# Attention sums made in a row, and softmax reciprocals spread by TensorE instead of GpSimd

## The chip, the cores and the metric

One core of one Trainium2 chip runs the whole program. The metric is the time of one execution on the device in microseconds (us), as the median of several runs. Engines are named as in the profile: PE is TensorE's matrix product, PEld its weight load, DVE is VectorE, ACT is ScalarE, POOL is GpSimd, SP is SyncE, whose queue issues transfers.

## The reference, cut to what matters

The input x has shape (4, 1024, 256). Four blocks are added to it one after the other, each on a layer norm of x: a linear recurrent unit, a sparse feed-forward block (the same weights are used twice), an attention block, and the feed-forward block again. The change lies in the attention:

```
q = (x @ Wq.T).reshape(b, t, 8, 64)
kv_latent = x @ Wkv_down.T
k = (kv_latent @ Wk_up.T).reshape(b, t, 8, 64)
v = (kv_latent @ Wv_up.T).reshape(b, t, 8, 64)
scores = einsum('bqhd,bkhd->bhqk', q, k) * 64 ** -0.5
attn = softmax(scores, axis=-1)
out = einsum('bhqk,bkhd->bqhd', attn, v)
return out.reshape(b, t, 512) @ Wo.T
```

Everything is float32. The output is x after all four blocks.

## The kernel before, in words

x stays in SBUF as 32 tiles of 128 tokens by 256. The program has three stages. Up to about 390 us it runs the recurrent unit, prepares the attention's weights and starts the first feed-forward block; from 392 to 1310 us it runs the attention, with the rest of the first feed-forward block (L589) and the preparation of later queries, keys and outputs woven in; then the second feed-forward block ends the program.

**Units of the attention.** `heads` (L857) goes over one batch in 32 units: two halves of the tokens (`nb`), four pairs of heads (`g`), four query tiles (`q`). With four batches that is 128 units. A unit has two steps, one for each head of the pair (`j`). A step makes scores of 128 queries by 1024 keys on TensorE (L887, four records), copies them with the sign turned into SBUF on VectorE while it takes the row minimum (L893, tile `pr`, four buffers; `nm` is the bias), and takes exponentials with their row sums on ScalarE (L896, row sums to `ssum`). The probabilities must then be transposed, so that keys lie on partitions.

**Two ways to transpose.** A DMA unit (`q` even) splits the probabilities into two float16 parts, by a cast on ScalarE (L899) and a difference on POOL (L900), in tile `pd` (two buffers), and SP issues a transposing transfer to `d0` or `d1` (L901, two buffers each). A TensorE unit (`q` odd) transposes float32 blocks on TensorE (L907) and copies them from PSUM to `p0` or `p1` (L912, mostly ScalarE, one buffer each).

**The sum of a unit.** `values_sum` (L922) is called later for a unit that is done. It takes reciprocals of the two row sums (L926, VectorE), spreads them over 2 x 64 columns on POOL (L928, `rows`), multiplies the transposed probabilities with the values on TensorE (L932: 48 records with float16 `lb` for a DMA unit, 32 records with float32 `la` for a TensorE unit), transposes `rows` (L940) into the second half of the same PSUM tile `pmo`, copies that half to `rb` (L942, ScalarE, one buffer) and multiplies both halves into `on` (L943, VectorE). `pmo` shares the two PSUM buffers of tag "s" with all products that are woven in. `rs`, `rows` and most small tiles come from a pool with two buffers.

**What sets the order.** `heads` keeps finished units in two lists. A TensorE unit is summed in step j == 0 of the unit after it, a DMA unit in step j == 1 of the next DMA unit. After each step `merge` (L965) lets woven-in work run by due times written by hand (L1189 to L1216). Tile's planner then orders the instructions of each engine by a simulated timeline; buffers and data become waits on semaphores. So each engine has one fixed order of instructions, which is known from the built program, and a waiting instruction holds up those behind it on its engine.

The functions that the change touches, with what calls them:

Of the kernel before, what the change touches and what calls it, by code (L numbers as in the profile page):

```python
# [10 lines left out]
F32 = mybir.dt.float32  # L11
# [10 lines left out]
P = 128  # L22
B = 4
# [7 lines left out]
HD = 64  # L31
PAIRS = HEADS // 2
# [741 lines left out]
class Attention:  # L774
# [82 lines left out]
    def heads(self, b, psum):  # L857

        nc, sp, wp = self.nc, self.sp, self.hp
        kh, kl, la, lb = self.k[b]
        late, pending = [], []
        for nb, g, q in (
            (nb, g, q)
            for nb in range(2)
            for g in range(PAIRS)
            for q in ((0, 2, 1, 3) if b == B - 1 and nb and g == PAIRS - 1 else range(4))
        ):
            by_dma = q % 2 == 0  # L870
            if g == 0:
                self.on[b, nb, q] = wp.tile([P, PAIRS, P], F32, tag=f"on{q}", name=f"on{q}")
            qs = self.qs[b, nb, g]
            ssum = sp.tile([P, 2], F32, tag="ssum", name="ssum", bufs=4)
            if by_dma:
                pts = [wp.tile([P, 2 * TPB, P], F16, tag=f"d{j}", name=f"d{j}", bufs=2) for j in range(2)]
                parts = ((0, lb[0]), (TPB, lb[0]), (0, lb[1]))
                terms = [(v[:, c, :], i + c) for c in range(TPB) for i, v in parts]
            else:
                pts = [wp.tile([P, TPB, P], F32, tag=f"p{j}", name=f"p{j}") for j in range(2)]  # L880
                terms = [(la[:, c, :], c) for c in range(TPB)]
            for j in range(2):
                sc = psum.tile([P, T], "sc", "sc")
                for i, kk in enumerate((kh, kl)):
                    for kb in range(2):
                        sl = slice(kb * 512, (kb + 1) * 512)
                        nc.tensor.matmul(  # L887
                            sc[:, sl], qs[:, j, q * P : (q + 1) * P], kk[:, sl], start=(i == 0), stop=(i == 1)
                        )
                nm = sp.tile([P, 1], F32, tag="nm", name="nm", bufs=4)  # L890

                pr = wp.tile([P, T], F32, tag="pr", name="pr", bufs=4)
                nc.vector.tensor_scalar(pr, sc, -1.0, FMAX, ALU.mult, ALU.min, accum_out=nm)  # L893
                if by_dma:
                    nc.vector.tensor_scalar(nm, nm, PSHIFT * math.log(2.0), None, ALU.add)  # L895
                nc.scalar.activation(pr, pr, AF.Exp, bias=nm, scale=-1.0, accum_out=ssum[:, j : j + 1])  # L896
                if by_dma:
                    pd = wp.tile([P, 2, T], F16, tag="pd", name="pd", bufs=2)
                    nc.scalar.copy(pd[:, 0, :], pr)  # L899
                    nc.gpsimd.tensor_tensor(pd[:, 1, :], pr, pd[:, 0, :], ALU.subtract)  # L900
                    nc.sync.dma_start_transpose(pts[j], pd.rearrange("p i k -> p (i k)"))  # L901
                else:
                    for half in range(2):
                        pt = psum.tile([P, 4, P], "t", "ptp")
                        for kk in range(4):
                            kc = 4 * half + kk
                            nc.tensor.transpose(pt[:, kk, :], pr[:, kc * P : (kc + 1) * P], self.ident)  # L907
                        dst = pts[j][:, 4 * half : 4 * half + 4, :]
                        if half == 0 and b == B - 1:
                            nc.vector.tensor_copy(dst, pt)  # L910
                        else:
                            nc.scalar.copy(dst, pt)  # L912
                if j == 0 and pending:
                    self.values_sum(*pending.pop(0), psum)
                if j == 1 and late and by_dma != (q > 0 and (b, nb, g) == (B - 1, 1, PAIRS - 1)):
                    self.values_sum(*late.pop(0), psum)
                yield
            (late if by_dma else pending).append((pts, terms, ssum, self.on[b, nb, q][:, g, :]))
        for args in late + pending:
            self.values_sum(*args, psum)  # L920

    def values_sum(self, pts, terms, ssum, on, psum):  # L922

        nc, sp = self.nc, self.sp
        rs = sp.tile([P, 2], F32, tag="rs", name="rs")
        nc.vector.reciprocal(rs, ssum)  # L926
        rows = sp.tile([P, 2, HD], F32, tag="rows", name="rows")
        nc.gpsimd.tensor_copy(rows, rs[:, :, None].to_broadcast([P, 2, HD]))  # L928
        po = psum.tile([P, 2, P], "s", "pmo")
        for n, (v, c) in enumerate(terms):  # L930
            for j in range(2):
                nc.tensor.matmul(  # L932
                    po[j * HD : (j + 1) * HD, 0, :],
                    v,
                    pts[j][:, c, :],
                    start=(n == 0),
                    stop=(n == len(terms) - 1),
                )

        nc.tensor.transpose(po[:, 1, :], rows.rearrange("p j d -> p (j d)"), self.ident)  # L940
        rb = sp.tile([P, P], F32, tag="rb", name="rb", bufs=1)
        nc.scalar.copy(rb, po[:, 1, :])  # L942
        nc.vector.tensor_tensor(on, po[:, 0, :], rb, ALU.mult)  # L943
# [383 lines left out]
```

## Time and profile before

| | |
|---|---|
| median of 3 runs | 1528.88 us (1526.93 to 1530.15) |
| the profiled execution | 1528.96 us |
| its span | 1527.2 us |
| PE busy, share of the span | 1291.6 us, 85% |
| DVE busy | 1194.9 us, 78% |
| ACT busy | 1025.3 us, 67% |
| POOL busy | 681.6 us, 45% |
| L928 on POOL (`rows`) | 128 copies, 37.3 us, mean 294 ns |
| L940 on PE (transpose of `rows`) | 128 records, mean 333 ns in the stage |
| L926 on DVE (reciprocals) | 128, mean 156 ns in the stage |
| L942 on ACT, L943 on DVE | 128 each, mean 266 and 285 ns in the stage |

A busy PE counts each record until its modelled end, and records overlap: a record's mean is its latency, and what a row of products costs is read from the distance of starts. A wait is idle time of an engine just before an instruction, put down to what released it. The chain of waits follows the work back from the last instruction, and so names what was late at each moment; work beside the chain could grow by its slack at no cost.

### The profile page before, as it was taken

To read this page: it belongs to the slowest core of one execution; us is meant where nothing else is said; L and a number is where in the kernel's file an instruction comes from. 1 tells how busy PE (TensorE), PEld (TensorE's weight loads), DVE (VectorE), ACT (ScalarE), POOL (GpSimd) and SP (SyncE) were. 2 spreads that over 40 slices of the span, in tenths; PEclk is the share of its full clock that TensorE was granted. 3 is DMA by queue.
4 is the path that set the end of the run, shared out by engine and by line. 5 is a ranking of instruction groups with operands and counts; after the bars stand their busy time and mean duration, and the time that the engine had idled before them with its cause. 6 is when DMAs were issued, how large, how long until landed. Compare 5 with 4: busy or idle time off the path is not lost.

```text
span 1527.2 us, 28862 instructions
## 1 busy us (share of the span) xinstructions
PE 1291.6 (85%) x10134; PEld 955.8 (63%) x10136; DVE 1194.9 (78%) x3938; ACT 1025.3 (67%) x2152; POOL 681.6 (45%) x849
## 2 busy tenths in 40 slices
PE   5879998697899888988888988889889999566766
PEld 3635455376677767756776766677777877344544
DVE  8976665697889777779778686877685775599998
ACT  5353433466889767887878777877777876566654
POOL 2033332162555444543544453444353544067775
PEclk9999999699999998999999899999999999679888
DMA  3010000321444343435344333534363445000000
GB/s 118 28 46 15 20 23 21 124 91 60 87 86 95 60 77 73 88 60 86 64 83 78 73 63 70 77 60 84 56 110 72 84 82 100 1 15 25 21 22 32
DMA packets 288612, 96.53 MB, mean 63 GB/s; under 512 B 268233, under 2 KB 284626, under 8 KB 288466
## 3 DMA queue, kind: packets, MB, share of 16 engines
q1 hardware_dynamic: 283024, 88.50, 28.9%
q10 hardware_dynamic: 5442, 6.18, 1.2%
q8 instruction: 80, 1.31, 0.3%
q14 instruction: 66, 0.54, 0.1%
HBM read 16.01 MB, written 11.53 MB: 18 GB/s over the span
## 4 chain that ended last, share of the span: by engine, by line
PE 34%; DVE 34%; ACT 16%; DMA 6%; issue 5%; POOL 4%; SPq 0%; ACTq 0%; POOLq 0%; DVEq 0%
DVE wk L674 8%; PE pmo L932 7%; DVE m L674 6%; PE sc L887 6%; DVE pr L893 6%; ACT pr L896 5%; DMA d<-pd 5%; PE po L437 3%; PE ptp L907 2%; ACT p L912 2%; ACT pd L899 2%; PE pmy L170 2%; PE pu L170 2%; DVE qs L854 2%; PE pz L452 1%
## 5 line engine op out<-in xcount | busy, mean ns | idle before, releaser
L900 POOL TENSOR_TENSOR pd<-pr,pd 128x1024 f16<-128x1024 f32 x128 | 274.3, 2145 | 196.0 <-ACT pd L899 152.1
L893 DVE TENSOR_SCALAR_CACHE_REDUCE pr<-sc 128x1024 f32<-128x1024 f32 x256 | 308.9, 1217 | 60.3 <-POOL pd L900 29.1
L896 ACT ACTIVATE pr<-pr,nm 128x1024 f32<-128x1024 f32 x256 | 294.5, 1152 | 57.2 <-DVE nm L895 38.8
L887 PE MATMUL sc<-kh,qs 128*128 128x512 f32 x512 | 184.4, 438 | 31.6 <-DVE pr L893 16.6
L907 PE MATMUL ptp<-ident,pr 128*128 128x128 f32 x1024 | 144.3, 277 | 24.7 <-ACT p L912 22.3
L887 PE MATMUL sc<-kl,qs 128*128 128x512 f32 x512 | 164.6, 401 | 0.0
L674 DVE MATCH_REPLACE8 wk<-m,wk 128x256 f32<-128x256 f32 x384 | 154.4, 405 | 0.1
L907 PEld LDWEIGHTS ptp<-ident,pr 128*128 128x128 f32 x1024 | 118.3, 142 | 54.2 <-ACT p L912 37.9
L674 DVE MAX8 m<-wk 128x8 f32<-128x256 f32 x384 | 149.9, 410 | 0.6
L912 ACT COPY p<-ptp 128x512 f32<-128x512 f32 x224 | 123.5, 587 | 40.0 <-PE pmo L932 29.8
L899 ACT CAST pd<-pr 128x1024 f16<-128x1024 f32 x128 | 133.6, 1046 | 24.8 <-DMA d<-pd 23.7
L932 PE MATMUL pmo<-p,la 128*64 128x128 f32 x2048 | 136.5, 284 | 4.3 <-DVE qs L854 2.9
L932 PEld LDWEIGHTS pmo<-p,la 128*64 128x64 f32 x2048 | 117.8, 141 | 23.1 <-issue 4.5
L887 PEld LDWEIGHTS sc<-kh,qs 128*128 128x128 f32 x512 | 85.4, 195 | 58.4 <-DVE pr L893 25.4
L628 POOL TENSOR_TENSOR ex<-ex,wk 128x512 f32<-128x512 f32 x61 | 77.9, 1277 | 79.8 <-DVE wk L674 64.9
L887 PEld LDWEIGHTS sc<-kl,qs 128*128 128x128 f32 x512 | 97.3, 191 | 22.7 <-issue 1.0
L932 PE MATMUL pmo<-d,lb 128*64 128x128 f16 x3072 | 101.6, 222 | 7.7 <-ACT ex L615 5.0
L932 PEld LDWEIGHTS <-lb 128*64 128x64 f16 x3072 | 91.4, 111 | 22.2 <-issue 19.0
L928 POOL COPY rows<-rs 128x128 f32<-128x128 f32 x128 | 37.3, 294 | 140.3 <-PE pmo L940 135.6
L699 PE MATMUL pf<-wf,vt 128*128 128x256 f32 x288 | 83.5, 432 | 4.4 <-ACT vt L697 3.6
L147 PE MATMUL pt<-ident,xn 128*128 128x128 f32 x256 | 50.0, 318 | 41.6 <-ACT xn L145 32.9
L556 PE MATMUL pl<-lint,xc_f 128*128 128x512 f32 x128 | 71.8, 648 | 10.4 <-ACT xc_f L587 10.4
(308 smaller groups left out, 2769.9 us busy)
## 6 DMA issues: line engine op xcount, KB each, us to landing
tt<-ft SPq DMA_DIRECT2D x16, 256.0 KB
tt<-tt SPq DMA_DIRECT2D x8, 512.0 KB
out<-x SPq DMA_DIRECT2D x32, 128.0 KB
x<-in_x ACTq DMA_DIRECT2D x6, 512.0 KB
pf<-pfs SPq DMA_DIRECT2D x12, 256.0 KB
full<-pf SPq DMA_DIRECT2D x24, 128.0 KB
d<-pd SPq DMA_TRANSPOSE x128
wa<-in_w_attn SPq DMA_DIRECT2D x2, 640.0 KB
```

What stands on the lines that cost most here:

```text
L556: self.last_logits = nc.tensor.matmul(v, x, w.lint, start=False, stop=True).ins
L628: pool.tensor_tensor(ex, ex, wk, ALU.subtract)
L674: ins = make(*args).ins
L699: nc.tensor.matmul(dst, vt[:, k, :], w.wf[:, k, :], start=(k == 0 and bias is None), stop=(k == KD - 1))
L887: nc.tensor.matmul(sc[:, sl], qs[:, j, q * P : (q + 1) * P], kk[:, sl], start=(i == 0), stop=(i == 1))
L893: nc.vector.tensor_scalar(pr, sc, -1.0, FMAX, ALU.mult, ALU.min, accum_out=nm)
L896: nc.scalar.activation(pr, pr, AF.Exp, bias=nm, scale=-1.0, accum_out=ssum[:, j : j + 1])
L899: nc.scalar.copy(pd[:, 0, :], pr)
L900: nc.gpsimd.tensor_tensor(pd[:, 1, :], pr, pd[:, 0, :], ALU.subtract)
L907: nc.tensor.transpose(pt[:, kk, :], pr[:, kc * P : (kc + 1) * P], self.ident)
L912: nc.scalar.copy(dst, pt)
L932: nc.tensor.matmul(po[j * HD : (j + 1) * HD, 0, :], v, pts[j][:, c, :], start=(n == 0), stop=(n == len(terms) - 1),)
```

## The change

Both sums are called at one place, in step j == 0 after a TensorE unit: first that of the waiting DMA unit, then that of the TensorE unit. The exception in the last group of the last batch is gone. In `values_sum` the tile `rows` and its POOL copy are gone; instead TensorE makes two float32 products, one for each head, in which the stationary operand is one column of `rs` seen 64 times and the moving operand the identity. `rs` has four buffers.

```
                 if j == 0 and pending:
-                    self.values_sum(*pending.pop(0), psum)
-                if j == 1 and late and by_dma != (q > 0 and (b, nb, g) == (B - 1, 1, PAIRS - 1)):
-                    self.values_sum(*late.pop(0), psum)
+                    for units in (late, pending):
+                        self.values_sum(*units.pop(0), psum)
                 yield
...
-        rs = sp.tile([P, 2], F32, tag="rs", name="rs")
+        rs = sp.tile([P, 2], F32, tag="rs", name="rs", bufs=4)
         nc.vector.reciprocal(rs, ssum)
-        rows = sp.tile([P, 2, HD], F32, tag="rows", name="rows")
-        nc.gpsimd.tensor_copy(rows, rs[:, :, None].to_broadcast([P, 2, HD]))
         po = psum.tile([P, 2, P], "s", "pmo")
...
-        nc.tensor.transpose(po[:, 1, :], rows.rearrange("p j d -> p (j d)"), self.ident)
+        for j in range(2):
+            nc.tensor.matmul(
+                po[j * HD : (j + 1) * HD, 1, :],
+                rs[:, j : j + 1].to_broadcast([P, HD]),
+                self.ident,
+                start=True,
+                stop=True,
+            )
         rb = sp.tile([P, P], F32, tag="rb", name="rb", bufs=1)
```

## The prediction

> **What bounds the kernel now.** I read the share of each engine in the attention stage first (all edits lie in it), then who waits for whom there, then the chain that ended last. The stage runs from 392 to 1310 us. Its row gives busy time of PE, weight loads, DVE, ACT and POOL, then granted clock, DMA share and GB/s:
>
> ```profile
> 392.00:1310.00 918.00, 822.86 (x8348) 654.49 (x8348) 695.50 (x1978) 707.43 (x1365) 427.49 (x418) 0.98 0.43 77
> ```
>
> No engine is full: TensorE idles 95 us, VectorE 222, ScalarE 211, POOL 491. Time is lost in waits between queues that each run in order. Columns: total us, times, longest.
>
> ```profile
> POOL rows L928 <- PE pmo L940: 135.6, 58, 8.4
> ...
> DVE rs L926 <- ACT pr L896: 30.6, 26, 3.8
> ACT p L912 <- PE pmo L932: 29.8, 15, 3.6
> DVE pr L893 <- POOL pd L900: 29.1, 22, 3.4
> ...
> ACT pd L899 <- DMA d<-pd: 23.7, 29, 3.0
> ...
> DVE pr L893 <- PE sc L887: 21.7, 29, 2.9
> ```
>
> And of SP's queue in the same stretch:
>
> ```profile
> SPq L901 <- PE pmo L932: 363.1, 52, 16.1
> ```
>
> The largest entries sit on POOL and SP, which have time to spare; what counts is what reaches ScalarE, VectorE and TensorE, and that is 20 to 30 us a row. The chain shows how it reaches them (start, us, what):
>
> ```profile
> 917.78 1.90 PE pmo L932 x32
> 919.67 0.26 PE pmo L940
> 919.94 0.58 PE pc L529 x4
> 920.52 1.14 PE sc L887 x4
> 921.66 0.89 PE ptp L907 x8
> 922.57 1.24 DVE pr L893 x2
> 923.86 1.21 PE sc L887 x4
> 925.07 1.46 PE pmo L932 x48
> 926.53 0.06 PE pmo L940
> 926.59 5.13 DMA d<-pd
> 931.80 1.05 ACT pd L899
> 932.88 0.08 issue
> 932.98 2.14 POOL pd L900
> 935.14 1.24 DVE pr L893 x2
> ```
>
> A sum of a DMA unit (48 records, 1.46 us) ends, and 0.06 us later a transfer starts that had waited for it: d has two buffers, so the transposes of one DMA unit need the sum of the DMA unit two before. Then the cast waits for pd, POOL for the cast, VectorE for pr. Over the stage the chain is 34% TensorE, 27% VectorE, 20% ScalarE, 8% DMA (15 pieces, 72 us). It passes L940 49 times of 128, the reciprocal of L926 26 times, rows 6 times.
>
> **The change, part by part.** I sum against the profiled execution: 1528.96 us, a span of 1527.2 and 1.76 around it, within 0.1 us of the median of 1528.88. I give each part the share of its waits or work that the chain makes likely, with both ends.
>
> *The DMA sums come earlier.* The late sum is called at j == 0, half a unit sooner. In the built program's TensorE order a DMA sum stands on average 9.4 score steps (a step is four records of L887) behind its own unit's last scores; after the change, 7.7. For ScalarE's first cast of a unit this means: the sum that frees d for the transfer it depends on stood 1.7 steps ahead of it, now 3.3. So SP's 363 us should mostly go, and with it the cast's wait of 23.7 us, the upper end. 15 of its 29 waits are in the chain: 15 x 0.82 = -12 us; ends -24 and 0. Could the sum now overtake its data? The sum of unit 12 was at 572 us, its second transfer was issued at 553 and such a piece takes some 5 us: 14 us to spare, 6 are taken. No new wait. SP's queue moves with it: its order stays transposes with the 24 loads of full between them, none is passed by much, and VectorE waited only 6.8 us behind full's chain.
>
> *No rows on POOL.* 128 copies of 0.294 us (37 us) and 135.6 us of waiting go. What stood behind a waiting copy? The cast's partner L900, and it was itself waiting for ScalarE in nearly all cases: only 8 times did it start late because of rows, 13.1 us in all. Upper end -13; by the chain's 6 visits, of which some two carry 1.6 us each, I take -3. The cover here is that POOL is 53% idle.
>
> *Two fp32 products in place of a transpose.* In the fence above 32 records of fp32 sums (16 products with 64 stationary columns) take 1.90 us, 0.119 each; 8 fp32 transposes take 0.89, 0.111 each. New: 2 x 0.119 = 0.238, against 0.111: +0.127 us, x 128 = +16 us on the engine with least idle time. The view with stride zero as stationary operand isn't in this trace; the nearest row, 64 columns of la, loads in 0.14 us beside the products, and I take the same for it. With 49 of 128 on the chain: +6 us; ends 0 and 16. Here two pages of the Trainium skill speak against the edit. "Perfetto Trace Analysis", section Transposes, asks that a logical transpose be done in transpose mode and not as a standard matmul; "FP8 and Floating Point Precision", section TensorE Precision Notes, gives a true fp32 product four passes through the array. Four passes of 0.111 for each of two products would be 0.89 us a sum, +0.78, or +100 us in all and +38 by the chain. The row decides: fp32 products with 64 columns stand in the trace as two records each, at 0.119 us a product, so the two halves cost twice a transpose and not eight times. I use +6.
>
> *The reciprocal is freed of rows and has four buffers instead of two.* It can be placed as soon as the planner thinks the exponentials done, and it is: with durations from the groups, the VectorE work between a unit's last L893 and its reciprocal falls from 5.9 us on average to 3.4, and reciprocals with under 3 us of such work rise from 27 to 64 of 128. The trace says what is needed: ScalarE's second row sum of a unit is there 2.56 us after VectorE ended that pr (1.2 to 4.7). So many more reciprocals will wait on VectorE, with the next L893, L674 and L943 queued behind them, and ScalarE, which needs nm of that L893, behind those. Price: in the trace 26 waits, 30.6 us, 1.18 each, which is about the 27 little-covered ones. For 64: 75 us, +45. VectorE holds 27% of the chain: +12 us. Ends 0 (it has 222 us of idle time) and +45.
>
> *Sums in a row.* In the order TensorE gets a DMA sum and a TensorE sum with no score between them 42 times, before 27. Such a pair is about 4 us without scores; VectorE's waits for sc average 0.75 us. 15 x 0.75 = 11, by VectorE's share +3; ends 0 and 11, or below if the pair frees pmo sooner than it did. In return p, which has one buffer, is freed in better time: ScalarE's first p copy stood at least one step ahead of the sum that frees it in 25 of 47 cases, now in 16. Its 29.8 us fall to 19; a quarter of the p copies (56 of 224) are in the chain: -3; ends -11 and 0. Reciprocal rows are read through rb with one buffer, so the second rb of a pair waits for the first L943; its distance in the two orders is nearly the same, and of the 15 added pairs' L943 of 0.285 us, 4 us in all, I take a quarter, +1 (ends -3 and +4). The last DMA sum of the kernel falls behind the last scores, but stands at the same place ahead of the last 16 records as before: 0.
>
> Sum: -12 - 3 + 6 + 12 + 3 - 3 + 1 = +4: 1528.96 + 4 = 1533 us.
>
> **The rivals.** *The transfers' relief wins (faster).* Here VectorE's new waits fall into time in which it would have waited for sc, rb or POOL anyway (222 us idle), and the whole of the cast's wait is won: -24 - 3 - 3 + 6 + 3 and +4 of the 45: -17, 1512 us. For it: 363 us on SP and the doubled distance of the sums. Against: ScalarE itself waited 23.7 us only, so that is all there is to win directly. It decides if less than some 20 us of the reciprocals' 45 land on the path; by VectorE's chain share 12 do, yet the relief must then come in full and not in its half.
>
> *The pair blocks the scores (slower).* If VectorE, with two sc tiles ahead at most, runs dry in each of the 15 added pairs, they cost a TensorE sum and its reciprocal, 1.9 + 0.24 us each: +32 instead of +3, 1562 us. For it: 21.7 us of waits for sc already. Against: 27 such pairs exist today at a mean wait of 0.75.
>
> *It does little where it counts.* rows and SP were idle time of engines with slack. Relief and TensorE's 16 us cancel, the reciprocals wait where nothing follows: 1529 us.
>
> **How the numbers follow.** A measurement of this kernel can tell about 0.2%, 3 us, from no change. Forecast (parts as summed, reciprocals on the path): 40%, own range 1532 to 1545. Pair blocks the scores: 10%, 1545 to 1562. Little where it counts: 15%, 1526 to 1532. Relief wins: 35%, 1505 to 1526. So faster 0.35, same 0.15, slower 0.50. The range takes in the relief down to 1509 and the forecast's upper end with half the blocked pairs, 1553.
>
> **What would show it.** In the changed profile: the wait of SP's transposes for the sums should fall from 363 us below 150, and the cast's 23.7 below 8; if not, the first step is wrong. The rows of POOL are gone, and L893's wait for POOL should fall, below 25. The new products should add about 16 us to TensorE's busy time; 100 would mean four passes. VectorE's wait at the reciprocal should rise from 30.6 to 60 or more; if it stays near 30, my forecast fails at that step and the relief wins. Waits for sc well above 35 us would speak for the blocked scores. A TensorE clock far from 0.98 in the stage would upset all of it.

## The result, and the profile after

The changed kernel takes 1555.72 us (median of 4 runs, 1555.03 to 1556.88) against 1528.50 for the kernel before in the same session: ratio 1.0182, 95% interval 1.0167 to 1.0197, so 27 us slower. The forecast was 1533 us, with a range up to 1553. The profiled execution has a span of 1555.2 us, against 1527.2.

First the row of the attention stage, which now lasts until about 1340 us (columns as before: PE, weight loads, DVE, ACT, POOL, granted clock, DMA share, GB/s):

```profile
392.00:1340.00 948.00, 842.38 (x8729) 675.05 (x8726) 707.70 (x1967) 705.10 (x1362) 393.52 (x289) 0.96 0.42 75
```

The stage has grown by 30 us. TensorE is busy 20 us longer, VectorE 12 us (with no more instructions), ScalarE no longer than before; all three idle more. Over the whole program TensorE's busy time rose by 17.2 us (1291.6 to 1308.8). That this lies near the predicted 16 is luck: e2_row below, without any of the new products, is busy 18.3 us longer than the kernel before.

The granted clock is 0.96 instead of 0.98 in this stage. Over whole executions it is 0.934 on average in the changed kernel, and 0.936 to 0.938 in the kernel before in five other sessions; there 0.001 less clock went with 0.3 to 1.0 us more time from one execution to another. By these numbers the lower clock goes with at most 3 of the 27 us, an estimate.

The waits in that stage (total us, times, longest):

```profile
ACT pr L896 <- DVE nm L895: 50.0, 34, 3.2
DVE rs L925 <- ACT pr L896: 41.8, 39, 2.7
ACT pr L896 <- DVE pr L893: 34.8, 33, 4.8
DVE pr L893 <- PE sc L887: 24.4, 30, 2.4
DVE pr L893 <- POOL pd L900: 22.1, 23, 4.9
...
ACT p L912 <- PE pmo L929: 17.7, 10, 3.2
DVE rs L925 <- PE pmo L938: 14.0, 10, 2.9
ACT pd L899 <- DMA d<-pd: 12.2, 8, 6.3
```

And SP's queue:

```profile
SPq L901 <- POOL pd L900: 251.4, 68, 12.8
SPq L901 <- PE pmo L929: 161.8, 31, 15.3
```

The first of these lines was, in the kernel before:

```profile
SPq L901 <- POOL pd L900: 74.3, 18, 10.2
```

The waits that were named fell: SP waits 162 us for the sums instead of 363, the cast 12.2 instead of 23.7, `p` 17.7 instead of 29.8, L893 22.1 for POOL instead of 29.1, and the 135.6 us of `rows` are gone. But SP now waits for POOL's difference instead (251 us, before 74): once the sums are out of the way, that comes last. What got worse on VectorE and ScalarE is small by comparison: the reciprocals wait 41.8 + 14.0 us instead of 30.6 (the 14.0 are new: with four buffers, `rs` is written again only when the products that read it are done), and ScalarE waits 50.0 + 34.8 us for VectorE where it was 38.8 + 15.3. By this table the change ought to have been about even. The chain of waits gives no help: in this trace it breaks off in the second feed-forward block.

```profile
DVE 9%; PE 6%; ACT 3%; issue 1%; POOL 1%; DMA 1%; ACTq 0%; POOLq 0%; DVEq 0%
```

The shares add up to 21% of the span; nothing of the attention can be read from it, and no stage chain for the changed kernel stands behind anything said below.

The new products are cheaper than predicted. In order of start (us, duration of the group, records):

```profile
907.95 1.53 PE L929 MATMUL pmo<-d,lb 128*64 128x128 f16 x48
...
909.32 0.39 PE L938 MATMUL pmo<-ident,rs 128*64 128x128 f32 x4
...
909.54 1.91 PE L929 MATMUL pmo<-p,la 128*64 128x128 f32 x32
...
911.28 0.39 PE L938 MATMUL pmo<-ident,rs 128*64 128x128 f32 x4
911.60 0.50 PE L887 MATMUL sc<-kl,qs 128*128 128x512 f32 x1
```

Both sums stand in a row with no score between. From 909.32 to 909.54 are 0.22 us for two products, four records. The kernel before has such a row in a few places:

```profile
1099.95 1.53 PE L932 MATMUL pmo<-d,lb 128*64 128x128 f16 x48
1101.41 0.33 PE L940 MATMUL pmo<-ident,rows 128*128 128x128 f32 x1
1101.67 1.97 PE L932 MATMUL pmo<-p,la 128*64 128x128 f32 x32
1103.57 0.33 PE L940 MATMUL pmo<-ident,rows 128*128 128x128 f32 x1
1103.66 0.71 PE L887 MATMUL sc<-kh,qs 128*128 128x512 f32 x2
```

From the first product of the two sums to the scores behind them the changed kernel takes 3.65 us (907.95 to 911.60) and the kernel before 3.71. The forecast set 0.11 us against the pair, the share of one transposition in a row of eight; but L940, alone between other products, took 0.26 us before another sum and 0.09 before scores. Counted from the last product of a sum to the start of what follows, over all kernels here and at the median, the two products take 0.13 us more than the transposition before scores, 0.05 more before another transposition, and 0.14 less before another sum. Over the changed kernel's sums, for which 118 of 128 can be matched in this way, that adds up to 2 us, and over those of e1_pair below to 5: estimates from the traces, against the forecast's 16.

**Where the time went.** The starts of the 256 exponentials (L896), in the one profiled execution of each kernel, give the time of each batch of 64 steps. That is the reading on which the experiments rest:

| us | before the first | batch 1 | batch 2 | batch 3 | batch 4 (63 steps) |
|---|---|---|---|---|---|
| before | 381.9 | 229.3 | 245.1 | 245.6 | 186.3 |
| after | 380.1 | 247.2 | 243.5 | 250.9 | 197.4 |

The loss is not spread over 128 sums. Batch 1 loses 18 us, batch 4 loses 11, the two in the middle 4 together. Batch 4 has no tiles of the first feed-forward block woven in; batches 1 to 3 have eight each. Its row before and after:

```profile
1101.80:1288.20 186.40, 177.71 (x1866) 144.32 (x1866) 135.69 (x333) 149.42 (x263) 86.50 (x71) 0.99 0.49 89
```

```profile
1121.70:1319.00 197.30, 183.55 (x1936) 149.20 (x1935) 138.91 (x333) 148.96 (x260) 80.25 (x42) 0.97 0.47 83
```

Here TensorE was busy 177.7 of 186.4 us, 95%. "TensorE idles 95 us" is a mean over the stage; in the last batch there were 9 us of idle time. After, it is busy for 5.8 us more and idle for 5.0 us more, 10.9 together.

### The profile page after: what moved, and what is told of

Read it like the earlier page. It is cut to its first block, busy times and chain, and to the rows that moved or that the text cites. A ratio compares the mean times of both kernels' runs of the same rounds, so it can differ in the third digit from the quotient of the medians.

```text
span 1555.2 us, 29475 instructions
## 1 busy us (share of the span) xinstructions
PE 1308.8 (84%) x10518; PEld 976.2 (63%) x10520; DVE 1208.7 (78%) x3938; ACT 1024.5 (66%) x2152; POOL 648.0 (42%) x721
## 5 line engine op out<-in xcount | busy, mean ns | idle before, releaser
L900 POOL TENSOR_TENSOR pd<-pr,pd 128x1024 f16<-128x1024 f32 x128 | 274.6, 2146 | 298.6 <-ACT pd L899 253.2
L893 DVE TENSOR_SCALAR_CACHE_REDUCE pr<-sc 128x1024 f32<-128x1024 f32 x256 | 310.1, 1217 | 56.6 <-PE sc L887 27.4
L896 ACT ACTIVATE pr<-pr,nm 128x1024 f32<-128x1024 f32 x256 | 294.4, 1152 | 89.7 <-DVE nm L895 50.0
L674 DVE MATCH_REPLACE8 wk<-m,wk 128x256 f32<-128x256 f32 x384 | 158.5, 418 | 0.2
L674 DVE MAX8 m<-wk 128x8 f32<-128x256 f32 x384 | 154.4, 424 | 0.4
L929 PE MATMUL pmo<-p,la 128*64 128x128 f32 x2048 | 133.4, 281 | 10.9 <-DVE qs L854 5.1
L899 ACT CAST pd<-pr 128x1024 f16<-128x1024 f32 x128 | 133.6, 1045 | 13.3 <-DMA d<-pd 12.2
L929 PE MATMUL pmo<-d,lb 128*64 128x128 f16 x3072 | 109.3, 228 | 6.9 <-ACT ft L524 2.9
L929 PEld LDWEIGHTS <-lb 128*64 128x64 f16 x3072 | 96.9, 115 | 21.4 <-issue 16.9
L947 DVE TENSOR_TENSOR on<-pmo,rb 128x128 f32<-128x128 f32 x128 | 36.7, 287 | 57.4 <-ACT rb L946 56.6
```

The lines of the kernel that those rows point to most:

```text
L674: ins = make(*args).ins
L929: nc.tensor.matmul(po[j * HD : (j + 1) * HD, 0, :], v, pts[j][:, c, :], start=(n == 0), stop=(n == len(terms) - 1),)
```

## The experiments

All times are medians. Each ratio is to runs of the kernel before on the same chip. "Batches" are the four numbers of the table above. Where an expectation names a theory by a letter: R is the forecast's main loss, reciprocals that come too early and hold VectorE up; T is that the order of woven-in work, fixed by due times written for the old order, no longer fits; W is that the change's own work costs the time whatever the due times.

### The two parts, each alone

**The pair of products alone, sums at their old places** (e1_pair):

```
-        rows = sp.tile([P, 2, HD], F32, tag="rows", name="rows")
-        nc.gpsimd.tensor_copy(rows, rs[:, :, None].to_broadcast([P, 2, HD]))
...
-        nc.tensor.transpose(po[:, 1, :], rows.rearrange("p j d -> p (j d)"), self.ident)
+        for j in range(2):
+            nc.tensor.matmul(
+                po[j * HD : (j + 1) * HD, 1, :],
+                rs[:, j : j + 1].to_broadcast([P, HD]),
...
```

> The kernel before with one part of the change: the two fp32 products take the place of rows and its transpose; sums stay at two places, rs keeps two buffers. In its built order DMA sums stand where they stood (9.4 steps behind their scores) and reciprocals late (12.8 us of VectorE work behind their L893, before 5.9). Theory P (the added TensorE work is the cost): 6 to 20 us over before. Theory R (early reciprocals stop VectorE): no wait at the reciprocal for ScalarE, so within 5 us of before. Theory S (sums in a row are the cost): within 5 us of before.

1550.07 us, ratio 1.0128 (1.0109 to 1.0148); batches 239.7, 249.6, 248.5, 193.8. The part that was to cost 3 us (+6 for the products, -3 for the missing `rows`) costs some 20.

**The sums in a row alone** (e2_row), with `rows`, the transposition and two buffers of `rs` kept:

```
-                    self.values_sum(*pending.pop(0), psum)
-                if j == 1 and late and by_dma != (q > 0 and (b, nb, g) == (B - 1, 1, PAIRS - 1)):
-                    self.values_sum(*late.pop(0), psum)
+                    for units in (late, pending):
+                        self.values_sum(*units.pop(0), psum)
```

> The kernel before with the other part: both sums at one place; rows, its transpose and two buffers of rs stay. DMA sums stand 7.9 steps behind their scores, 39 pairs have no score between them, and reciprocals stand early (3.9 us of VectorE work, 54 with under 3). Theory P: no loss, or a gain, as the cast's wait for transfers goes (0 to -20 us). Theory R: slower by 10 to 25 us, with VectorE's wait at the reciprocal at 40 us or more. Theory S: slower by 15 to 27 us, with more waits for scores and for pmo, whatever the reciprocals do.

1563.41 us, ratio 1.0212 (1.0172 to 1.0252); batches 244.4, 255.4, 249.6, 201.6. Alone it costs 33 us, more than both parts together (its four executions took 1554.68 to 1568.25 us, and the profiled one 1567.24). So the parts do not add, and each alone is bad. Its busy times in us (share of the span, instructions), without one new product:

```profile
PE 1309.9 (84%) x10134; PEld 968.8 (62%) x10136; DVE 1198.1 (77%) x3938; ACT 1026.8 (66%) x2152; POOL 681.8 (44%) x849
```

TensorE is busy 18.3 us longer than in the kernel before. So busy time depends on the order too, and a rise of 17 us does not show what the new products cost. The waits of its stage:

```profile
ACT pr L896 <- DVE nm L895: 57.3, 45, 3.4
DVE pr L893 <- POOL pd L900: 38.8, 26, 4.8
DVE pr L893 <- PE sc L887: 38.7, 42, 2.7
...
DVE rs L925 <- ACT pr L896: 22.4, 22, 2.4
...
DVE rs L925 <- POOL rows L927: 14.0, 8, 2.9
```

Here VectorE does wait 38.7 us for scores, where it was 21.7: the forecast's rival of the pair that blocks the scores, in the kernel without the new products. In the changed kernel the same line stands at 24.4.

### Reciprocals and buffers

**More buffers for `rs`** (e3_rs12: 12 instead of 4) and **fewer** (e4_rs2: 2, as before), each in the changed kernel:

```
-        rs = sp.tile([P, 2], F32, tag="rs", name="rs", bufs=4)
+        rs = sp.tile([P, 2], F32, tag="rs", name="rs", bufs=12)
```

```
-        rs = sp.tile([P, 2], F32, tag="rs", name="rs", bufs=4)
+        rs = sp.tile([P, 2], F32, tag="rs", name="rs")
```

> The changed kernel with twelve buffers of rs in place of four. In the changed kernel VectorE waited 14.0 us at the reciprocal for the product that reads the buffer (L938). Theory R in its narrow form (four buffers run out): this wait goes, 5 to 14 us under the changed kernel. Theories P and S: within 5 us of the changed kernel, 1551 to 1561.

> The changed kernel with two buffers of rs. Reciprocals then stand late (10.8 us of VectorE work, 8 with under 3), the sums as in the changed kernel. Theory R: the wait for ScalarE at the reciprocal goes from 41.8 to under 10 us, and 10 to 25 us of the loss with it, 1531 to 1546, unless waits for L938 take its place. Theories P and S: no gain, 1551 to 1561.

With 12 buffers 1563.18 us, ratio 1.0212 (1.0196 to 1.0228); with 2, 1543.88, ratio 1.009 (1.0075 to 1.0106). Batches: 245.0, 253.4, 250.5, 195.9 and 241.2, 245.6, 242.8, 197.5. Freer reciprocals are worse, by 20 us from end to end. That looked like R, but R has to pass the next run.

e4_rs2 differs from e1_pair by the sums in a row alone, both with two buffers of `rs`. There the row wins 6 us: 1543.88 against 1550.07, and the intervals of the ratios lie apart.

**Reciprocals late, four buffers** (e5_late): in the changed kernel each reciprocal is held behind the last L893 that the program issued before the sum was called.

```
-        nc.vector.reciprocal(rs, ssum)
+        with self.tc.issue_after(self.last_pr):
+            nc.vector.reciprocal(rs, ssum)
```

> The changed kernel with each reciprocal held in VectorE's order behind the L893 of the step in which its sum is called; four buffers of rs stay. VectorE work between a unit's last L893 and its reciprocal rises from 3.4 to 6.7 us, reciprocals with under 3 us fall from 64 to 23; sums and products stay. Theory R (waits at the reciprocal): the 41.8 us of waits for ScalarE fall below 15, the waits for the products (14.0) stay or shrink, and 8 to 18 us of the loss go: 1538 to 1548. Theories P and S, and theory T (the due times written by hand fit the order before and no other): within 5 us of the changed kernel, 1551 to 1561.

1553.54 us, ratio 1.0163 (1.0136 to 1.0191): 2 us less than the changed kernel, which the intervals do not tell from nothing. Its waits in the stage (the line numbers are one higher from the reciprocal on):

```profile
ACT pr L896 <- DVE nm L895: 51.4, 34, 4.1
DVE pr L893 <- POOL pd L900: 48.0, 38, 2.5
DVE pr L893 <- PE sc L887: 37.9, 38, 2.6
ACT pr L896 <- DVE pr L893: 33.9, 33, 4.8
...
DVE rs L926 <- PE pmo L939: 4.6, 3, 2.3
```

The 55.8 us of waiting at the reciprocals are down to 4.6, and 39 of these 51 us came back on the same engine: L893 waits 86 us for POOL and for scores instead of 46.5. ScalarE waits for VectorE as before (85.3 us against 84.8). So R falls: this wait was a place where VectorE waited, not a reason why it was late. What e4_rs2 won is then not explained by it.

**Four buffers with the pair alone** (e6_pair_rs4: e1_pair with `bufs=4` at `rs`).

> The kernel before with the two fp32 products and four buffers of rs; sums at two places. Reciprocals stand as in the kernel before (5.4 us of VectorE work, before 5.9; 34 with under 3, before 27), DMA sums too (9.4 steps). So little but TensorE's work and the lost rows differs from before. Theory P: 6 to 20 us over before. Theory R: within 6 us of before. Theory T: some 10 to 20 us over before, as any new order costs that.

1552.87 us, ratio 1.0155 (1.0131 to 1.018), against 1550.07 with two: the buffers of `rs` make 3 us where the sums stand apart, which the intervals do not tell from nothing, and 12 where they stand in a row.

### How much a pair costs, and whether `rows` mattered

**The pair made twice** (e7_twice), in the changed kernel. The second pass writes the same values again, so the result is unchanged.

```
-        for j in range(2):
+        for j in (0, 1, 0, 1):
```

> The changed kernel with each of the two products made twice, the second over the first: another 128 x 2 products of 0.119 us, 30 us of TensorE work. The order is otherwise near (DMA sums 7.7 steps, reciprocals 3.4 us). Theory P: the added work lies on the path by 38 to 100%, 1567 to 1586. Theories R, S and T: it is hidden by more than half, under 1567.

1574.93 us, ratio 1.03 (1.0277 to 1.0323): 19.2 us for a second pair. At 0.22 to 0.24 us for a pair, 128 pairs are 28 to 30 us of work, so about two thirds of this work came out as time. The forecast had 49 of 128, 38%. But it is no weight of each sum: the batches are 244.9, 256.9, 255.0 and 198.6, so of some 7 us of added work in each batch -2, +13, +4 and +1 us came out. In batch 4, where TensorE has least idle time, it was 1.2 us.

**The pair from `rows`, with the copy on POOL kept** (e9_pair_rows): in the kernel before only the transposition is replaced, and the stationary operand is `rows[:, j, :]`.

```
-        nc.tensor.transpose(po[:, 1, :], rows.rearrange("p j d -> p (j d)"), self.ident)
+        for j in range(2):
+            nc.tensor.matmul(
+                po[j * HD : (j + 1) * HD, 1, :],
+                rows[:, j, :],
...
```

> The kernel before with the two fp32 products in place of the transpose, but reading rows, which POOL still makes; all else stays, sums, reciprocals (5.6 us of VectorE work, before 5.9) and buffers. Beside the run that dropped rows too (1550.1) it parts TensorE's work from the lost rows. Theory P: 10 to 20 us over before, all of that run's loss. Theory V (without rows in its queue POOL works at other times, and reciprocals wait for TensorE on VectorE instead of rows on POOL): within 6 us of before.

1555.91 us, ratio 1.0183 (1.0152 to 1.0214); batches 243.9, 252.4, 245.4, 193.9. So neither the missing `rows` nor the view of stride zero is what costs; with `rows` it is 6 us slower than without (e1_pair), in the direction of the predicted -3.

**A third buffer of `rows` and four of `rs`, with the sums in a row** (e10_row_rows3) **and in the kernel before** (e11_rows3):

```
-        rs = sp.tile([P, 2], F32, tag="rs", name="rs")
+        rs = sp.tile([P, 2], F32, tag="rs", name="rs", bufs=4)
...
-        rows = sp.tile([P, 2, HD], F32, tag="rows", name="rows")
+        rows = sp.tile([P, 2, HD], F32, tag="rows", name="rows", bufs=3)
```

> The kernel with both sums at one place and rows on POOL (1563.4), with three buffers of rows and four of rs. If there POOL's waits for the transpose (82.3 us, with L900 behind them) and the reciprocal's wait for rows (14.0 us) are the cost, they fall below 40 and 5 us and the time to 1535 to 1550. If the place of the sums is the cost (theory S), it stays at 1556 to 1570; by theory R too, as reciprocals stand earlier (3.1 us of VectorE work, before 3.9).

> The kernel before with three buffers of rows and four of rs, nothing else. POOL's wait for the transpose (135.6 us) should halve. Theory R: reciprocals stand earlier (4.8 us of VectorE work, 47 with under 3), so VectorE's wait there rises and the time by 4 to 12 us. If POOL's waits are the greater cost: 3 to 10 us faster than before, the fastest of all kernels so far.

1558.16 us, ratio 1.0185 (1.0154 to 1.0215), and 1534.07, ratio 1.0028 (1.0014 to 1.0042). In a row `rows` had been short of buffers (the 14.0 us are gone, though the wait for scores is now 44.6), but that is worth at most 5 us of the 33, within the intervals. And the same two buffers, for which the kernel before has little use, cost it 5 us: part of such a difference is the newly planned order alone.

### The due times

`merge` lets the eight feed-forward tiles of batch 1 begin 6.75 steps apart, a number written for the old order. One edit, made to several kernels:

```
-            start = 1 + 6.75 * n if n < TPB else STEPS * (n // TPB) - STEPS + 48.25 + 8 * (n % TPB + 1)
+            start = 1 + 6.5 * n if n < TPB else STEPS * (n // TPB) - STEPS + 48.25 + 8 * (n % TPB + 1)
```

In the **kernel before** (e8_due) and in the **changed kernel** (e12_after_due):

> The kernel before with one due time of woven-in work changed: the feed-forward tiles of the first batch come 6.5 steps apart, not 6.75. Nothing is added or taken away, and the positions of sums and reciprocals stay within 0.2 us and 0.1 steps. It measures what a new order alone does. Theory T: 8 to 20 us slower, in the first batch. Theories P, R and S: within 5 us of before.

> The changed kernel with the same due time moved as in the control of the kernel before (tiles 6.5 steps apart), which cost that one 5 us, 4 of them in the first batch. Theory T (the due times fit the old order only): other times can win back much of the first batch's 18 us here, so this moves by 5 us or more, and rather down. Theories P and R: within 5 us of the changed kernel.

The kernel before becomes slower, 1534.58, ratio 1.0027 (1.0012 to 1.0041). The changed kernel becomes faster, 1540.57, ratio 1.0075 (1.0048 to 1.0102): 15 of the 27 us are back. Its batches are 230.6, 250.1, 243.8, 196.5: of the 18 us of batch 1 one is left, and batch 4 is as it was.

The trace shows what moved. In the 16 steps from 48 on, the changed kernel needed 84 us and the one with 6.5 needed 69. VectorE's groups in these windows, changed kernel first (line, engine, operation, shapes, count, busy us and mean ns, idle before):

```profile
L674 DVE MATCH_REPLACE8 wk<-m,wk 128x256 f32<-128x256 f32 x18 | 7.3, 408 | 0.0
...
L662 DVE TENSOR_TENSOR x<-x,pf 128x256 f32<-128x256 f32 x3 | 1.2, 406 | 0.0
```

```profile
L674 DVE MATCH_REPLACE8 wk<-m,wk 128x256 f32<-128x256 f32 x12 | 4.9, 410 | 0.0
...
L662 DVE TENSOR_TENSOR x<-x,pf 128x256 f32<-128x256 f32 x2 | 0.8, 412 | 0.0
```

L662 closes a feed-forward tile: three tiles end in these steps with 6.75, and two with 6.5, where the third was done earlier, in time that cost nothing: step 48 is reached at 543.2 us with five tiles done, and at 541.6 us with six. The kernel before also ends three tiles there, in 77 us. And what TensorE and ScalarE waited for in the two windows:

```profile
PEld ptp L907 <- ACT p L912: 7.6, 5, 3.9
...
ACT pd L899 <- DMA d<-pd: 6.3, 1, 6.3
PE ptp L907 <- ACT p L912: 5.7, 4, 3.8
```

None of these three lines is among the waits of the kernel with 6.5 there. The row of sums is not what makes the difference: e1_pair, whose sums stand apart, needs 79.6 us for these steps, and 68.8 with 6.5. By stretches of 16 steps, batch 1 is:

| us, from step | 0 | 16 | 32 | 48 |
|---|---|---|---|---|
| before, 6.75 | 51.8 | 40.9 | 59.5 | 77.0 |
| before, 6.5 | 51.9 | 44.4 | 66.4 | 70.8 |
| changed, 6.75 | 48.1 | 50.6 | 64.5 | 84.0 |
| changed, 6.5 | 47.0 | 50.8 | 64.3 | 68.6 |

Two tiles in place of three shorten the last stretch in both kernels, by 6 and 15 us; the kernel before loses 10 us for it in the 32 steps ahead, and the changed kernel nothing. So of the 18 us of batch 1 only 7 lie in the last stretch. Another 15 lie in steps 16 to 47, where 6.5 changes nothing in the changed kernel, and 4 are won back in the first 16 steps. Why those 32 steps take 115 us in the changed kernel, and 100 in the kernel before with 6.75 alone, no run shows.

**The same edit to each part alone** (h1_pair_due: e1_pair; h5_row_due: e2_row) **and to the changed kernel with two buffers of `rs`** (h4_rs2_due: e4_rs2), and **the other direction**, 7 instead of 6.75, in the changed kernel (h2_after_7). By the due times, 7 puts the end of the last of the eight tiles (57) behind the preparation that reads it (56), so that keys of batch 2 are made from x before the block is added to it and the output is wrong; the work is the same.

> The kernel before with the two fp32 products in place of rows and transposition (sums still at separate places), and with the due times of the first batch's woven-in tiles 6.5 steps apart instead of 6.75. Theory W (the pair costs TensorE work at each sum, at any order): the loss of some 20 to 27 us against the kernel before stays, 1548 to 1556. Theory T (the pair's cost is that due times written for the old order no longer fit): a good part of the first batch's loss goes, as it did when the changed kernel got 6.5; 1530 to 1540, first batch about 232 us instead of 240.

> The kernel before with the sums made in a row alone (rows and transposition kept) and due times 6.5 apart. Theory T: its first batch falls from 244 to about 232 us and the time from 1563 to about 1548. Theory W for the row (both sums together block TensorE for VectorE whatever is woven in): stays at 1558 to 1565.

> The changed kernel with two buffers of rs and due times 6.5 apart, the two edits that each won back 12 to 15 us of the 27. If they win at different things they add up: 1528 to 1533, level with the kernel before. If both only shuffle the same order, they don't add: 1538 to 1545.

> The changed kernel with due times 7 steps apart instead of 6.75 (the twin of the run with 6.5, in the other direction). If 6.5 helped because the woven-in work of the first batch is better earlier, 7 is slower than the changed kernel, 1560 or more. If any new order has a fair chance to lie better because the changed one lies badly, 7 helps as well: 1540 to 1550.

| kernel | 6.75 | 6.5 |
|---|---|---|
| before | 1528.50 | 1534.58, 1.0027 (1.0012 to 1.0041) |
| pair alone | 1550.07 | 1540.62, 1.0075 (1.0051 to 1.0098) |
| sums in a row alone | 1563.41 | 1540.95, 1.0092 (1.0068 to 1.0116) |
| changed | 1555.72 | 1540.57, 1.0075 (1.0048 to 1.0102) |
| changed, two buffers of `rs` | 1543.88 | 1533.38, 1.003 (1.001 to 1.005) |

Each kernel with a part of the change gains 9 to 22 us by an edit that costs the kernel before 4 to 6, and 7 helps the changed kernel as well (1541.15, ratio 1.0088, 1.0065 to 1.0111; batch 1 in 230.9). At 6.5 the parts alone and the whole are level, 6 us above the kernel before with the same due times (7 to 10 by the ratios). The two edits that help add up: with two buffers of `rs` and 6.5, the change costs 4.6 us against the kernel before as it stood and nothing that can be told against it with 6.5. Here too the row of sums wins 7 us where the pair has two buffers (1533.38 against 1540.62). None of these kernels beats the kernel before.

**A third value, 6.25, in both** (h7_before_625, h6_after_625), to see which of the two lay oddly at 6.75:

> The kernel before with due times 6.25 steps apart. With 6.75 and 6.5 it takes 1528.5 and 1534.6. If the kernel before is robust against when the woven-in tiles come due, 1530 to 1537; if 6.75 was a lucky place for it, 1540 or more.

> The changed kernel with due times 6.25 apart. If 6.75 is a bad place for the changed order and others are ordinary, 1537 to 1545, as with 6.5 (1540.6) and 7 (1541.2); and its distance from the kernel before with the same 6.25 is what the change itself costs, some 6 us (Theory T). If the change itself costs 20 us and more whatever the due times (Theory W), 1550 or more.

The kernel before takes 1529.61 us, ratio 0.9999 (0.9985 to 1.0012), so its place was no lucky one. The changed kernel takes 1546.65, ratio 1.0111 (1.0084 to 1.0137). Dividing the ratios at equal due times (1.0075 by 1.0027, and 1.0111 by 0.9999), the change costs 7 us with 6.5 and 17 with 6.25, where it cost 27 with 6.75: T is right that much of the 27 hangs on the due times, but wrong that the change would be free with other ones, and W is right that a cost stays, but wrong that it is 20 us and more in every order.

**What stays in every order is batch 4**, which this edit doesn't touch:

| | batch 4, us, by kernel |
|---|---|
| no part of the change (before, e8, e11, h7) | 186.3, 187.8, 187.0, 186.4 |
| pair alone (e1, e6, e9, h1) | 193.8, 191.5, 193.9, 190.4 |
| sums in a row alone (e2, e10, h5) | 201.6, 195.6, 198.6 |
| both (after, e3, e4, e5, e12, h2, h4, h6) | 197.4, 195.9, 197.5, 195.1, 196.5, 194.1, 197.1, 196.2 |
| both, the pair made twice (e7) | 198.6 |

The first two groups overlap with no other. The pair costs 4 to 8 us here, both parts 8 to 11. The rows of batch 4 with the pair alone (h1_pair_due), and with the sums in a row alone (h5_row_due):

```profile
1114.20:1304.60 190.40, 179.33 (x1966) 147.61 (x1962) 135.37 (x331) 149.73 (x262) 79.27 (x41) 0.99 0.52 89
```

```profile
1106.90:1305.50 198.60, 184.26 (x1873) 146.30 (x1871) 133.81 (x332) 149.99 (x260) 87.17 (x71) 0.97 0.47 83
```

In the first, batch 4 is 4.1 us longer than before. The forecast's 0.127 us for each of 32 pairs would also be 4 us, but TensorE is busy only 1.6 us longer there and idles 2.4 us more. With twice the pairs (e7), some 7 us of added work, batch 4 is 1.2 us longer than in the changed kernel. So it is not shown that the products' own work makes these 4 us.

In the second, which has no new product, TensorE is nevertheless busy 6.6 us longer, with 7 records more, and idles 5.6 us more. Its clock is 0.97 instead of 0.99; if that stretched all of 177.7 us it would make 3.7 of the 6.6, an estimate from the two rows. Whether the clock fell because of the pauses, or the pauses grew by the clock, no run tells apart. VectorE's waits for scores in batch 4, in the kernel before, with the row alone (h5_row_due) and in the changed kernel:

```profile
DVE pr L893 <- PE sc L887: 9.3, 10, 2.9
DVE pr L893 <- PE sc L887: 17.0, 18, 2.1
DVE pr L893 <- PE sc L887: 5.1, 8, 1.2
```

So the row alone blocks scores, but in the changed kernel these waits fell. What rose there are VectorE's waits for POOL's difference (5.6 to 11.4 us) and ScalarE's for VectorE (12.9 to 20.5). What the 8 to 11 us of batch 4 come from stays open.

## Why the prediction was wrong

The sign was right, the size was not: +4 us forecast, +27 measured. The step that failed is one that the sum put at nothing: it took the planned order as given. But each edit makes the planner set a new order for all engines, and the woven-in work meets it by due times written for the old one. Moving these due times alone makes the change cost 27, 7 or 17 us, so 10 to 20 us of the 27 hang on them. The second step that failed is the reciprocals: they waited as forecast, but that wait is not what their four buffers cost. Step by step:

- **What had no term at all.** With 6.75 batch 1 is 18 us slower than in the kernel before, with 6.5 it is 3 us faster than the kernel before with 6.5; that is more than any term of the sum. A range that allowed for it would have reached past 1553. Nor does 1553 follow from its own words, "the forecast's upper end with half the blocked pairs": 1545 and half of 32 us make 1561.
- **DMA sums earlier, -12.** By its own test the step is half right: SP's wait fell from 363 to 162 us (below 150 was asked for), the cast's from 23.7 to 12.2 (below 8), and most of SP's moved to POOL's difference (74 to 251 us). Where the sums stand apart (e1_pair, e9_pair_rows) the cast still waits 30.2 and 40.0 us, so the earlier sums did what was said of them. As time, the row of sums won 6 and 7 us (with 6.75 and 6.5) when it was added to the pair with two buffers of `rs`; with four buffers it cost 3 us, within the intervals, and added to the kernel before it cost 33 and 6. The relief alone was not isolated, since the same edit makes the row.
- **No rows on POOL, -3.** In keeping with e9_pair_rows against e1_pair (6 us), as far as two orders can tell.
- **Two products, +6.** The work was set too high. The pair takes 0.22 to 0.32 us, about the forecast 0.24, but the transposition that goes is worth more than the 0.11 us set against it: like for like, the change adds an estimated 2 us to TensorE's work, not 16. That the busy time rose by 17.2 us is luck, as e2_row rose by 18.3 without the products. As time the pair alone cost 20 us at the old due times and 6 at others, more than its work in both, so the weight "With 49 of 128 on the chain" was not tested. "No engine is full: TensorE idles 95 us" was a mean over a stage whose last batch had 9 us of idle time; that this is why the pair costs 4 to 8 us there is not shown.
- **What the pages said of the products.** The rule that speaks against the edit, to make a transposition as a transposition and not as a standard product (the Trainium skill, "Perfetto Trace Analysis", section Transposes), agrees with the traces before scores (0.13 us more) and not between two sums (0.14 us less). The row in the prediction does not speak against the four passes: a float16 product with the same 64 columns took 0.030 us there (1.46 for 48), the float32 one 0.119, 3.9 times as much. What was wrong in the 100 us is 0.111 us as the price of one pass.
- **Reciprocals, +12.** They did wait longer, 55.8 us against 60 or more forecast, and four buffers instead of two do cost 12 us (e4_rs2; 7 with 6.5). The agreement is luck: taking 51 us of the wait away with four buffers kept (e5_late) gave 2 us, within the intervals. The wait stood in for waits that come anyway. How the four buffers cost it is open.
- **Sums in a row, +3.** Too small for the row alone: waits for scores rose to 38.7 us, and the last batch costs 9 to 15 us more. The rival of the pair that blocks the scores named that mechanism, with +32, at 10%. In the changed kernel these waits are 24.4 us in the stage and 5.1 in the last batch, so there it is not the cause.
- **p copies -3, rb +1.** The first fell from 29.8 to 17.7 us of waiting; neither was tested as time.

Of the 28 us between the two profiled spans, 18 lie in batch 1, 11 in batch 4, and -1 in the start, the middle and the end of the program. Two edits take 22 of the 27 us back, two buffers of `rs` (12) and 6.5 (another 10). Batch 4 hangs on neither: against the kernel before with the same due times it costs 11, 9 and 10 us with 6.75, 6.5 and 6.25. That 6.25 takes 6 us more than 6.5 in the changed kernel (batches 1 and 3 at 234.4 and 252.8 against 230.6 and 243.8, batch 2 at 242.0 against 250.1) is scatter of new orders that no run here explains.

## What to carry to other kernels

When an order is planned anew and other work is woven in by due times written by hand, compare at several due times before a small edit is judged; here the same change cost 27, 7 and 17 us. For the same reason a busy time that rises by the forecast amount proves nothing by itself: look at a kernel that has a new order and none of the added work. Price an operation that is taken out in its own place, from the product before it to the one behind it, and not from a row of its kind. Read the share of each engine batch by batch, not over a stage. A long wait in front of one instruction is worth only what is left when it has moved: hold the instruction back once, and see whether the time or only the name of the wait changes.

## What the runs showed of the hardware that was not expected

- A float32 product with one column of a tile, seen 64 times with stride zero, as the stationary operand loads and runs like any other: 137 ns a load and 273 ns a record at the median in the changed kernel, and the same 137 and 273 ns from a written tile (e9_pair_rows).
- A single float32 transposition between sums took 0.26 us before the next sum and 0.09 us before scores, while eight in a row took 0.111 us each; two products in its place took 0.22 and 0.32 us.
- The granted clock of TensorE went with the order: over 392 to 1310 us it was 0.98 in the kernel before, 0.96 in the changed kernel, 0.95 with 12 buffers of `rs` and 0.99 in h4_rs2_due, with almost the same work.
- One VectorE operation, L636 (128x256, float32), took between 478 and 2386 ns within the changed kernel's stage (477 to 2366 in the kernel before). In all nine cases of the changed kernel over 2 us POOL's L900 was running when it began, and it ended 0.28 us after L900 did. No run moves the two apart.
